# A fused graph network on one core: pair 1's GRU products in the plain form

## The chip, the cores and the metric

The kernel runs on one core of a Trainium2 chip. The metric is the device time of one execution in microseconds (us); times are medians over several runs. The engines are PE (TensorE, with its weight loads shown as PEld), DVE (VectorE), ACT (ScalarE), POOL (GpSimd), and SP (SyncE), which here only issues DMAs.

## The reference

64 graphs of 256 nodes with 256 features each (float32), and a 0/1 adjacency matrix per graph. Four layers, each a normalization, a ReLU and a residual around one graph network: three of attention, and one gated graph network of three steps, which alone matters here:

```
for i in range(3):
    m = einsum('bnd,de->bne', h, weight[i])
    aggr = einsum('bst,bsd->btd', A, m)
    h = gru_cell(aggr, h, w_ih, w_hh, b_ih, b_hh)
# gru_cell
r = sigmoid(i_r + h_r); z = sigmoid(i_z + h_z)
n = tanh(i_n + r * h_n)
h = (1 - z) * n + z * h
```

Here `i_r, i_z, i_n` are the three thirds of `aggr @ w_ih.T + b_ih`, and `h_r, h_z, h_n` those of `h @ w_hh.T + b_hh`.

## The kernel before, in words

**Units.** `graphs(u, first, nb)` states the work of one unit. There are 33: u=0 is graph 0 alone (nb=1), u=1 to 31 are pairs of graphs (nb=2), u=32 is the last graph alone. For each unit it states three attention layers (`layer0`, `layer1`, `layer2`) and `gru`. Features lie on the 128 partitions in DC=2 blocks; the S = 256 nb nodes of the unit lie along the free dimension.

**What sets the order.** Nothing is issued where it is stated. Each step is an operation of a planner, `_Schedule`, with an engine, a cost in ns, the buffers that it reads and writes, and flags [...]. `paths` gives each operation a due time, backward from the end of its unit (PACE ns for two graphs). `play` runs the program forward in a model: each engine takes the ready operation that is due first, and one for whose buffers no slot is free is held back. Up to seven rounds follow, each with due times from a backward pass (`latest`) over the last plan; the plan with the shortest modelled span is issued, each engine in exactly that order. So an edit to one unit lays the whole program anew. Buffers come from classes with fixed numbers of slots (lines 893 to 903): `g` has 13, `ht3_` (the GRU's state, transposed) 2, `ag` 2, `am_r`, `hn` and `turn` 1, `sw` 3, PSUM banks 8.

**Setup.** Lines 1028 to 1048 multiply `weight[i]` into `w_ih` (`wc`, two thirds of whose columns are the r and z gates). Line 1054 forms sums and differences of gate weights: `s3` and `sh` stay in SBUF, `s[0..2]` of each layer go to DRAM (`sd`) and are fetched again as `sw` (line 1611). Setup operations have no unit of their own: they are due when the first operation that needs them is.

**A GRU layer.** `aggregate` (line 1471) multiplies the state's rows, split in a high and a low part (`hl`, line 1458), by the adjacency; the result is `ag`. Then come the gates, in one of two forms, then per block j the transposes back to rows (`rows_of`, line 1501), which feed the next layer's split.

The plain form (`plain(j, ...)`) takes each gate as it stands: for each block j twelve matmuls of S columns (`gate`, line 1486): r and z from `whh` and `wi`, n's two parts apart. Four ACT steps, five DVE steps. It needs four `g` buffers and four banks for each j, and writes the new state to another `ht3_` buffer, `h_new`.

The shared form uses that a pair holds two right-hand sides, and takes seven block products for eight, as in Strassen's scheme:
- `t1` is the difference of the two graphs' states (one DVE step).
- `hidden` (matmuls at line 1566) forms n's hidden part: three differences on DVE (line 1563), seven matmuls of 256 columns, four ACT steps, three additions on DVE.
- `products` (matmuls at line 1623) forms r and z: three `sw` loads on SP, three differences (line 1615), seven products of four 256-column matmuls each, three ACT copies, three additions.
- `unit(j, ...)` ends the gates: one 512-column gate (two matmuls), five ACT steps of which four are of one graph, four DVE steps; the state is written in place.

Steps issued through the helper `vec` show line 913 in the profile, whatever they are.

Of the kernel before, what the change touches and what calls it, by code (L numbers as in the profile page):

```python
# [2 lines left out]

# [514 lines left out]
SLOPES = (0.2, 0.01, 0.2)  # L518
SPREAD = 3
PACE = 93800  # L520


def _runs(numbers):
# [22 lines left out]
class _Schedule:  # L546
# [33 lines left out]
    def buf(self, cls, shape, dtype=F32, tile=None):  # L580
        return _Buf(cls, shape, dtype, tile)
# [229 lines left out]
def _fast_path(  # L811
# [38 lines left out]
    P = 128  # L850
    DC = D // P
    C = 2 * N // P
    S = 2 * N
# [50 lines left out]
    buf, op = sched.buf, sched.op  # L904
# [7 lines left out]
    def vec(fn, cost, *args, reads=(), writes=(), engine="dve", port=False, **kw):  # L912
        emit = lambda: fn(*[a() if callable(a) else a for a in args], **kw)  # L913
        op(engine, cost, emit, reads, writes, port=port)
# [173 lines left out]
    def graphs(u, first, nb):  # L1088

        C = 2 * nb  # L1090
        S = nb * N
# [44 lines left out]
        def transposed(xn, cls):  # L1136
            ht = buf(cls, [P, DC, S])

            def block(dc):
                ps = bank()  # L1140

                def emit():
                    for c in range(C):
                        nc.tensor.transpose(  # L1144
                            ps.tile[:, c * P : (c + 1) * P], xn.tile[:, c, dc * P : (dc + 1) * P], ident
                        )

                op("pe", pe(445), emit, [xn], [ps], takes=[ht])
                vec(nc.scalar.copy, act(600), lambda: ht.tile[:, dc, :], lambda: ps.tile[:, :S],
                    reads=[ps], writes=[(ht, dc)], engine="act")  # L1150

            for dc in range(DC):
                block(dc)
            return ht
# [294 lines left out]
        def gru(pair):  # L1449
# [65 lines left out]
            ht = transposed(hn, "ht3_")  # L1515
# [2 lines left out]
                aggregate(ag, split(lambda dc=dc: hn.tile[:, :, dc * P : (dc + 1) * P], [hn], True), dc)  # L1518
            for i in range(L):
                last = i == L - 1  # L1520
                h_new = ht if nb == 2 else buf("ht3_", [P, DC, S])
                wi = wc[:, i]
                stt = nc.vector.scalar_tensor_tensor

# [158 lines left out]
                        op0=OP.mult, op1=OP.subtract, reads=[d, n], writes=[(ht, j)], port=True)  # L1683

                half = 0.5 if i == 0 else 0.25
                if nb == 2:
                    t1 = buf("g", [P, DC, N])
                    vec(nc.vector.tensor_tensor, 700, lambda t1=t1: t1.tile, lambda ht=ht: ht.tile[:, :, N:],
                        lambda ht=ht: ht.tile[:, :, :N], op=OP.subtract, reads=[ht], writes=[t1], port=True)
                    ns = hidden(ht, t1)  # L1690
                    rz = products(i, ht, t1, ag, wi)
                    for j in range(DC):
                        unit(j, ht, ag, wi, half, ns[j], *rz)
                else:
                    for j in range(DC):
                        plain(j, ht, ag, h_new, wi, half)
# [5 lines left out]
                ht = h_new  # L1702
# [4 lines left out]
        layer1(pair)  # L1707
        layer2(pair)
        gru(pair)


    for u, (first, nb) in enumerate(units):
        sched.group = u
        sched.end[u] = (first + nb) * PACE / 2
        graphs(u, first, nb)
# [3 lines left out]
    sched.group = U  # L1719
    sched.end[U] = sched.end[-1] = (B / 2 + 1) * PACE  # L1720
    good, bad = buf("rs", [P, 64]), buf("rs", [P, 1])
# [66 lines left out]
```

## Time and profile before

| | |
|---|---|
| median of 3 runs | 3045.0 us (3042.98 to 3045.96) |
| the profiled execution | 3046.62 us, its span 3044.8 us |
| PE busy | 2974.3 us |
| DVE busy | 2606.7 us |
| ACT busy | 2124.8 us |
| granted PE clock, mean | 0.991 |

A line of the profile names the source line, the engine, the operation, and "out<-in" by tile names without their numbers: `bank` is PSUM, `pt` attention weights, `ht` the transposed features or state, `ag` the aggregate, `g` a scratch tile. Busy time is the union of an engine's instructions; matmuls are pipelined, so their durations overlap. Each float32 matmul of the program is two MATMUL records. A wait is put down to what ended last before the waiting instruction started. Windows count from the start of the span.

Where the early units stand: the first GRU product of pair 1 (u=1) is at 149.6 us on PE, those of graph 0 (u=0) at 174.7 us where they need only the state, and at 247 us where they need its aggregate, those of pair 2 (u=2) from about 298 us.

### The profile page before, as it was taken

To read this page: it belongs to the slowest core of one execution; us is meant where nothing else is said; L and a number is where in the kernel's file an instruction comes from. 1 tells how busy PE (TensorE), PEld (TensorE's weight loads), DVE (VectorE), ACT (ScalarE), POOL (GpSimd) and SP (SyncE) were. 2 spreads that over 40 slices of the span, in tenths; PEclk is the share of its full clock that TensorE was granted. 3 is DMA by queue.
4 is the path that set the end of the run, shared out by engine and by line. 5 is a ranking of instruction groups with operands and counts; after the bars stand their busy time and mean duration, and the time that the engine had idled before them with its cause. 6 is when DMAs were issued, how large, how long until landed. Compare 5 with 4: busy or idle time off the path is not lost.

```text
span 3044.8 us, 58325 instructions
## 1 busy us (share of the span) xinstructions
PE 2974.3 (98%) x21458; PEld 2478.7 (81%) x21458; DVE 2606.7 (86%) x6310; ACT 2124.8 (70%) x4997; POOL 425.4 (14%) x643
## 2 busy tenths in 40 slices
PE   8699999999999999999999999999999999999998
PEld 7588787888888888888888888888888888888887
DVE  7877788988988888988888988888988888988774
ACT  7566577776777776677777777777777777776554
POOL 3301101111111011111011111011111011111000
PEclk9799999999999999999999999999999999999999
DMA  5111122212212212212222222211222221211110
GB/s 146 40 62 44 55 81 78 81 54 84 74 64 84 84 54 80 74 65 83 84 67 69 72 67 84 84 70 64 70 70 81 84 72 62 67 63 59 49 42 28
DMA packets 150946, 212.56 MB, mean 70 GB/s; under 512 B 49238, under 2 KB 102012, under 8 KB 143228
## 3 DMA queue, kind: packets, MB, share of 16 engines
q1 hardware_dynamic: 146752, 207.40, 21.3%
q8 instruction: 172, 2.82, 0.4%
q10 hardware_dynamic: 3900, 1.34, 0.2%
q14 instruction: 122, 1.00, 0.1%
HBM read 180.62 MB, written 19.68 MB: 66 GB/s over the span
## 4 chain that ended last, share of the span: by engine, by line
PE 90%; DVE 6%; ACT 1%; DMA 1%; POOL 1%; SPq 1%; issue 0%; ACTq 0%; DVEq 0%; POOLq 0%
PE bank L1623 34%; PE bank L1486 12%; PE bank L1166 11%; PE bank L1275 11%; PE bank L1566 9%; PE bank L1471 6%; PE bank L1144 4%; PE bank L1501 3%; DVE o L913 1%; DVE g L913 1%; DVE pt L913 1%; SPq L1352 1%; PE bank L1203 1%; DMA sw<-sd 1%; ACT pt L1256 1%; DVE mean L913 0%
## 5 line engine op out<-in xcount | busy, mean ns | idle before, releaser
L913 ACT ACTIVATE g<-bank,bg 128x256 f32<-128x256 f32 (+1 forms) x780 | 395.3, 522 | 222.0 <-PE bank L1623 100.1
L1256 ACT ACTIVATE pt<-cb,f 128x256 f32<-128x256 f32 x1062 | 465.0, 504 | 99.9 <-PE bank L1275 99.6
L913 DVE SCALAR_TENSOR_TENSOR pt<-pt,f,cap 128x256 f32<-128x256 f32 x1152 | 487.7, 477 | 18.1 <-ACT pt L1256 12.8
L1275 PEld LDWEIGHTS bank<-wh,pt 128*64 128x64 f32 (+1 forms) x8704 | 347.7, 141 | 73.5 <-issue 46.7
L1275 PE MATMUL bank<-wh,pt 128*64 128x65 f32 (+1 forms) x8704 | 396.0, 232 | 7.5 <-DVE pt L913 6.7
L1486 PE MATMUL bank<-ag,wc 128*128 128x512 f32 (+1 forms) x888 | 383.1, 561 | 0.0
L913 ACT ACTIVATE g<-g,bg 128x256 f32<-128x256 f32 x570 | 267.1, 502 | 133.3 <-DVE g L913 105.2
L1623 PE MATMUL bank<-g,sw 128*128 128x256 f32 x1488 | 351.5, 379 | 0.0
L913 ACT COPY g<-bank 128x512 f32<-128x512 f32 x279 | 163.1, 585 | 252.0 <-PE bank L1623 234.3
L1623 PEld LDWEIGHTS bank<-g,sw 128*128 128x128 f32 x1488 | 282.7, 190 | 38.6
L1486 PEld LDWEIGHTS bank<-ag,wc 128*128 128x128 f32 x888 | 160.6, 190 | 106.9 <-issue 95.4
L1118 POOL TENSOR_SCALAR mv<-mv 128x4 f32<-128x4 f32 (+1 forms) x132 | 48.0, 364 | 1409.9 <-DVE mv L1110 1131.3
L1471 PE MATMUL bank<-am_r,hl 128*128 128x256 f32 x1536 | 235.1, 299 | 0.8 <-DVE am_r L913 0.4
L913 DVE TENSOR_TENSOR g<-bank,g 128x512 f32<-128x512 f32 x279 | 190.3, 683 | 37.4 <-PE bank L1623 20.7
L1127 ACT ACTIVATE xn<-xt,mv 128x256 f32<-128x256 f32 x384 | 208.9, 598 | 10.9 <-DVE mv L913 10.5
L1109 DVE BATCH_NORM_STATS2 st<-xt 128x6 f32<-128x256 f32 x512 | 208.6, 407 | 7.7 <-DMA xt<-in_x_dram 7.4
L1471 PEld LDWEIGHTS bank<-am_r,hl 128*128 128x128 f32 x1536 | 202.4, 189 | 10.6 <-DVE hl L913 1.1
L1623 PE MATMUL bank<-ag,sw 128*128 128x256 f32 x744 | 179.1, 384 | 7.7 <-DVE g L913 4.1
L1623 PE MATMUL bank<-ag,wc 128*128 128x256 f32 x744 | 179.4, 384 | 0.7 <-ACT ag L913 0.7
L1623 PE MATMUL bank<-ht,whh 128*128 128x256 f32 x744 | 178.7, 384 | 0.8 <-ACT ht L913 0.8
L1623 PE MATMUL bank<-g,s 128*128 128x256 f32 x744 | 176.1, 380 | 0.0
L1623 PE MATMUL bank<-g,wc 128*128 128x256 f32 x744 | 175.9, 379 | 0.0
(128 smaller groups left out, 5892.7 us busy)
## 6 DMA issues: line engine op xcount, KB each, us to landing
sw<-sd SPq DMA_DIRECT2D x279, 256.0 KB, 2.6
cb<-rd SPq DMA_DIRECT2D x58, 1024.0 KB, 4.6
xt<-in_x_dram SPq DMA_DIRECT2D x31, 512.0 KB, 3.7
at<-in_adj_dram SPq DMA_DIRECT2D x31, 512.0 KB, 6.0
out_dram<-xt SPq DMA_DIRECT2D x31, 512.0 KB, 3.0
cb<-rd SPq DMA_DIRECT2D x29, 256.0 KB, 3.3
sd<-g SPq DMA_DIRECT2D x9, 256.0 KB, 2.3
cap<-cap_n SPq DMA_TRANSPOSE x128, 2.4
```

Source lines behind the costliest of these rows:

```text
L913: emit = lambda: fn(*[a() if callable(a) else a for a in args], **kw)
L1109: nc.vector.bn_stats(st.tile[:, c, :], xt.tile[:, c, :])
L1127: op("act", 610, lambda: nc.scalar.activation(xn.tile[:, c, :], xt.tile[:, c, :], AF.Relu, bias=mv.tile[:, 3, c : c + 1], scale=mv.tile[:, ...
L1144: nc.tensor.transpose(ps.tile[:, c * P : (c + 1) * P], xn.tile[:, c, dc * P : (dc + 1) * P], ident)
L1166: nc.tensor.matmul(ps.tile[:, : heads * W], lhsT=ht.tile[:, dc, c * P : (c + 1) * P], rhs=we[:, dc].rearrange("p h w -> p (h w)"), start=( ...
L1256: op("act", 500, lambda: nc.scalar.activation(pt.tile[:, b, jc, :], source(h, b), AF.Exp, scale=slope - 1.0, bias=f.tile[:, 1, h, c : c + ...
L1275: nc.tensor.matmul(ps[q * Q : (q + 1) * Q], lhsT=pt.tile[:, b, jc, i0 : i0 + Q], rhs=wh.tile[:, h, 2 * b + jc, :w], start=(jc == 0), stop= ...
L1471: nc.tensor.matmul(ps.tile[:, b * N : (b + 1) * N], lhsT=hl.tile[:, k, 2 * b + sc, :], rhs=am.tile[:, 2 * b + sc, :], start=(k == 0 and sc ...
L1486: nc.tensor.matmul(ps.tile[:, :S], lhsT=w[:, dc, g * P : (g + 1) * P], rhs=v.tile[:, dc, :], start=(first and dc == 0), stop=(last and dc ...
L1501: nc.tensor.transpose(ps.tile[:, c * P : (c + 1) * P], ht.tile[:, j, c * P : (c + 1) * P], ident)
L1566: op("pe", 432, lambda: nc.tensor.matmul(ps.tile[:, where], lhsT=w, rhs=v(), start=first, stop=False, skip_group_check=True,), [*reads, B_ ...
L1623: nc.tensor.matmul(ps.tile[:, j * N : (j + 1) * N], lhsT=w()[:, dc, j * P : (j + 1) * P], rhs=view()[:, dc], start=(first and j == 0 and d ...
```

## The change

The pair u=1 takes the plain form in all three GRU layers, with S = 512, and a second `ht3_` buffer for its new state. Pairs u=2 to 31 keep the shared form; graphs 0 and 63 were plain already. The setup is unchanged, but its sums are first needed by u=2. The added import is not used.

```diff
+import random
...
 SPREAD = 3
 PACE = 93800
+PLAIN = 2
...
             for i in range(L):
                 last = i == L - 1
-                h_new = ht if nb == 2 else buf("ht3_", [P, DC, S])
+                h_new = ht if nb == 2 and u >= PLAIN else buf("ht3_", [P, DC, S])
                 wi = wc[:, i]
...
                 half = 0.5 if i == 0 else 0.25
-                if nb == 2:
+                if nb == 2 and u >= PLAIN:
                     t1 = buf("g", [P, DC, N])
...
                     ns = hidden(ht, t1)
                     rz = products(i, ht, t1, ag, wi)
                     for j in range(DC):
                         unit(j, ht, ag, wi, half, ns[j], *rz)
                 else:
                     for j in range(DC):
                         plain(j, ht, ag, h_new, wi, half)
```

## The prediction, made before the changed kernel was run

> **What bounds the kernel now.** I read the page first (busy times, the 40 slices, the granted clock), then the waits of PE, then windows of the first 500 us, then the timeline of the longest gap.
>
> ```profile
> span 3044.8 us, 58325 instructions
> ...
> PE 2974.3 (98%) x21458; PEld 2478.7 (81%) x21458; DVE 2606.7 (86%) x6310; ACT 2124.8 (70%) x4997; POOL 425.4 (14%) x643
> ...
> PE   8699999999999999999999999999999999999998
> ...
> PEclk9799999999999999999999999999999999999999
> ```
>
> PE (TensorE) is idle for 3044.8 - 2974.3 = 70.5 us in all, and the slices put nearly all of that into the first two or three (76 us each). The windows of 500 us from 1000 to 2500 have PE busy 499.2, 498.7 and 498.9. So a microsecond of PE work added anywhere lengthens the kernel by a microsecond, unless a gap takes it up, and the gaps worth having lie before 500 us. The change concerns graphs 1 and 2 (unit u=1), and their GRU stands in just that region: its first product on PE starts at 149.6 us, the last write of its state is at about 321. The windows there (columns: stretch; busy PE, PEld, DVE, ACT, POOL; granted clock; DMA share; GB/s):
>
> ```profile
> core 0: us, PE busy (x) PEld busy (x) DVE busy (x) ACT busy (x) POOL busy (x), PEclk, DMA share, GB/s
> ...
> 150.00:160.00 10.00, 10.00 (x48) 8.78 (x48) 9.79 (x24) 5.65 (x12) 2.98 (x6) 1.00 0.38 133
> 160.00:170.00 10.00, 7.74 (x92) 6.54 (x91) 9.93 (x27) 10.00 (x26) 0.00 (x0) 1.00 0.22 55
> ...
> 220.00:228.00 8.00, 7.93 (x98) 6.84 (x97) 7.93 (x25) 4.01 (x10) 0.00 (x0) 1.00 0.07 26
> 228.00:233.00 5.00, 0.00 (x0) 0.00 (x1) 5.00 (x14) 5.00 (x14) 0.00 (x0) 0.88 0.00 2
> 233.00:240.00 7.00, 6.33 (x18) 5.07 (x19) 6.81 (x19) 4.08 (x14) 1.52 (x2) 0.50 0.01 2
> ...
> 320.00:334.00 14.00, 10.88 (x43) 7.02 (x42) 12.37 (x32) 5.79 (x12) 3.33 (x3) 1.00 0.17 43
> ```
>
> The reader is to see that where PE stops, DVE (VectorE) is full: 9.79 and 9.93 of 10 us around the gap at 163 us, 5.00 of 5 in the gap at 228, and that the clock is 0.50 after the longer gap. The waits of PE over the whole kernel (total us, times, longest):
>
> ```profile
> PE bank L1144 <- ACT xn L1127: 30.6, 2, 16.8
> ...
> PE bank L1566 <- ACT ag L913: 5.1, 1, 5.1
> ...
> PE bank L1623 <- DMA sw<-sd: 3.1, 6, 0.7
> ```
>
> The 30.6 us are the load at the very start (13.8) and the gap from 88 to 105 us (16.8), both before this GRU. The 5.1 us are one wait of pair 1's GRU, and the timeline of ACT, DVE and PE shows what stands in it:
>
> ```profile
> 225.52 6.48 ACT L1256 ACTIVATE pt<-cb,f 128x256 f32<-128x256 f32 x16
> ...
> 232.37 0.57 ACT L913 COPY ag<-bank 128x512 f32<-128x512 f32 x1
> ```
>
> ```profile
> 226.41 6.42 DVE L913 SCALAR_TENSOR_TENSOR pt<-pt,f,cap 128x256 f32<-128x256 f32 x16
> ...
> 233.94 0.69 DVE L913 TENSOR_TENSOR hl<-bank,hl 128x512 fp32r<-128x512 f32 x1
> ```
>
> ```profile
> 233.00 2.08 PE L1566 MATMUL bank<-ht,whh 128*128 128x256 f32 x4 [5.07 <-ACT ag L913]
> ```
>
> Sixteen attention weights of a later pair sit on ACT and DVE ahead of the two small steps that feed the third GRU layer, and PE has nothing else ready.
>
> [...]
>
> **The change, part by part.** Three layers of one pair leave the shared form (`hidden`, `products`, `unit`) for `plain`. Each product is two records in the trace. From the chain of work:
>
> ```profile
> 195.23 1.73 PE bank L1623 x8
> ...
> 210.45 3.43 PE bank L1486 x8
> ```
>
> A 256-column record takes 1.73/8 = 0.216 us, one of 512 columns 3.43/8 = 0.429.
>
> PE: the shared form has 7 products of four 256-column matmuls (56 records), `hidden` 7 matmuls (14) and two 512-column gates (8): 70 x 0.216 + 8 x 0.429 = 18.6 us. Plain has 24 matmuls of 512 columns, 48 x 0.429 = 20.6. Added: 2.0 us a layer, **6.1 us** in all. This is certain, and hidden only if it fills a gap.
>
> DVE and ACT, from the groups (the second number after the bar is the mean ns of one):
>
> ```profile
> L913 DVE TENSOR_TENSOR g<-bank,g 128x512 f32<-128x512 f32 x279 | 190.3, 683 | 37.4 <-PE bank L1623 20.7
> ...
> L1563 DVE TENSOR_TENSOR g<-ht,g 128x256 f32<-128x256 f32 x6 | 2.5, 412 | 0.0
> ```
>
> ```profile
> L913 ACT ACTIVATE g<-g,bg 128x256 f32<-128x256 f32 x18 | 8.5, 501 | 3.4 <-DVE g L913 3.4
> ...
> L913 ACT ACTIVATE g<-bank,bg 128x512 f32<-128x512 f32 x4 | 2.7, 687 | 3.0 <-PE bank L1486 3.0
> ```
>
> DVE per layer: shared 15 steps of 512 elements and 6 of 256, 15 x 0.684 + 6 x 0.415 = 12.8 us; plain 10 x 0.684 = 6.8. Saved 5.9, or 5.0 if each is counted by its distance to the next (0.60 and 0.33): **15 to 18 us** in three layers. ACT per layer: shared 6 x 0.470 + 6 x 0.501 + 2 x 0.687 + 3 copies x 0.585 = 9.0; plain 6 x 0.687 and two from SBUF, which the trace lacks at 512 elements (I take 0.72[...]): 5.6. Saved 3.4, **10 us** in all. Neither engine ends the kernel, so this is worth only what it closes of PE's gaps.
>
> What it closes. (a) DVE issues three of the sums for the weight differences (L1054) at 105 to 107 us inside a DVE-led piece of the chain. Pair 1 no longer needs them, so they can fall later: 3 x 0.60 = 1.8 us, at least 0. (b) Between 149 and 165 us DVE is full, with 4.3 us of layer 0's differences and additions by 160 us; plain has at most two steps (1.2) there, so some 3 us less, and the 2.26 us gap goes: 2.3. (c) The gap at 228: 5.07 us, 0.67 at 237, and the half clock behind it (4 records in 2.08 for 0.86, 8 aggregates in 1.72 for 0.94, 16 records in 5.97 for 3.46): 4.5 us. Together 10.3. With 10 to 12 us less DVE work before it, in two layers, the weights can stand ahead of the layer's end instead of inside it. I take all of it; zero is the other end, because the order is the planner's and not DVE's load. Sum: 6.1 - 1.8 - 2.3 - 10.3 = **-8.3 us**.
>
> Costed at nothing: nine `sw` loads on SP (256 KB, 2.6 us to land) and the wait for them. PE's waits from 105 to 500 us name no `sw`, so nothing shortens[...]. The state: plain writes h_new to another of two `ht3_` slots. The single graph 0 already does so while pair 1 holds the other slot, and its two final writes then stand together (262.2, 280.5, 297.5 us), waiting for the last reader of the old state: a few tenths of a us of DVE order, hidden while PE has other pairs' attention. If that cover is gone, it is the second rival of the slower side.
>
> The working is against the profiled execution (3046.62 us, span 3044.8). The median of the runs shown is 3045.0, 1.6 us (0.05%) lower; I put the difference on the median: 3045.0 - 8.3 = 3036.7, so **3037**.
>
> **The rivals.** First, the gaps move but half remain: the planner lays the whole program anew, and a wait like (c) appears at another place. For it: the 320 to 334 us window and 473 us show more such gaps, in pairs that don't change. Against: DVE's load does fall. (a), (b) and a quarter of (c) cover the 6.1: about 3045. Second, slower: PE has its fill anyway. From 170 to 228 us PE is idle under 0.1 us, so the added work there is paid in full, and if (c) is an order and no load, nothing pays it back: 3045 + 6.1 = 3051; it decides if the GRU's aggregation still stands behind a block of 16 weights. Third, the slots: pair 2's transposes already come at 307 us, though its split was at 286.8. If pair 1 in plain form holds both slots, pair 2's GRU isn't there as filler; one more gap like (c) costs 9.6 us or so on top: 3061. That the edit does nothing is excluded: the test on `u` is plainly met by unit 1.
>
> **How the numbers follow.** Chances: forecast 0.45 (own range 3028 to 3041, the low end if the gap after 320 us, 3.7 us and its half clock, goes too), half remain 0.22, full price 0.18, slots 0.15. A difference under 0.2% (6 us) can't be told from none. Faster by more: 0.45 less 0.05 above 3039, 0.40. Within: 0.05 + 0.22 + 0.04 = 0.31. Slower: 0.14 + 0.15 = 0.29. The range from 3028 to 3057 leaves out most of the slot case and a little below.
>
> **What would show it.** PE busy up by some 6 us less the half-clock time; DVE down 15 to 18, ACT about 10; `sw` loads 270 for 279[...]. I am wrong if the gap between two layers of pair 1 is still there, if a longer gap stands elsewhere before 500 us, or if the early gap at 88 us changes: I have left that alone, since nothing of this GRU runs before it.

## The result, and the profile after

The changed kernel takes 3016.94 us (median, 3014.51 to 3018.15) against 3044.55 us of the kernel before beside it: ratio 0.9907, 95% interval 0.9892 to 0.9923, some 28 us faster. The forecast was 3037 in a range from 3028 to 3057: the direction was right, the size a third of what was measured, and the time lies below the range.

From the page of the kernel after, these lines answer to those shown of before (line numbers are 2 higher than before):

```profile
span 3016.3 us, 58014 instructions
...
PE 2971.5 (99%) x21368; PEld 2454.4 (81%) x21368; DVE 2595.9 (86%) x6277; ACT 2118.2 (70%) x4970; POOL 425.8 (14%) x643
...
PE   8899999999999999999999999999999999999998
...
PEclk9899999999999999999999999999999999999999
```

PE is idle for 3016.3 - 2971.5 = 44.8 us, 25.7 less than the 70.5 of before. Its busy time fell by 2.8 us although the plain form adds 6.1 us of work; that leaves 8.9 us, put down to less time at a granted clock of 0.50. In windows of 1 us it is 0.50 from 89 to 112, 137 to 143, 232 to 242, 335 to 341 and 475 to 477 us before, and from 86 to 88, 113 to 116 and 120 to 129 us after; its mean is 0.996 for 0.991. The windows bear this out as an estimate: PE's busy time times the missing share of the clock, summed over windows up to 600 us, is some 15 us before and 5 after. 25.7 + 2.8 = 28.5, the difference of the spans.

The same windows as in the prediction, of the kernel after:

```profile
core 0: us, PE busy (x) PEld busy (x) DVE busy (x) ACT busy (x) POOL busy (x), PEclk, DMA share, GB/s
...
160.00:170.00 10.00, 10.00 (x60) 8.50 (x59) 8.30 (x35) 8.21 (x19) 3.72 (x7) 1.00 0.01 2
...
228.00:233.00 5.00, 5.00 (x29) 4.23 (x28) 5.00 (x11) 4.45 (x10) 4.69 (x4) 1.00 0.16 34
233.00:240.00 7.00, 7.00 (x43) 5.32 (x42) 6.86 (x19) 2.61 (x6) 1.25 (x2) 1.00 0.08 16
...
320.00:334.00 14.00, 14.00 (x45) 8.36 (x44) 13.29 (x35) 6.22 (x11) 6.66 (x6) 1.00 0.07 20
```

All gaps that the prediction wanted closed are closed, and the one at 320 us too. But the waits of PE show a second change, which the prediction had left out (total us, times, longest one):

```profile
PE bank L1146 <- ACT xn L1129: 17.5, 5, 9.7
...
PE bank L1625 <- DMA sw<-sd: 2.2, 6, 0.8
```

The wait for `xn`, the normalized input, is 13 us shorter (30.6 before), and the single gap of 16.8 us is gone. It stood at 88 to 105 us, long before pair 1's GRU. It is not gone without a trace: one wait for `xn` of 7.3 us now stands at 116 us. Coarser windows, first of the kernel before, then of the one after, show how the gain is spread:

```profile
80.00:140.00 60.00, 36.02 (x357) 30.21 (x354) 50.86 (x152) 28.33 (x69) 19.66 (x25) 0.77 0.15 46
140.00:240.00 100.00, 91.98 (x656) 76.76 (x655) 82.45 (x208) 71.01 (x172) 13.16 (x19) 0.94 0.16 51
240.00:345.00 105.00, 100.01 (x695) 84.03 (x695) 82.74 (x201) 61.87 (x146) 19.73 (x26) 0.96 0.16 46
345.00:600.00 255.00, 249.83 (x1864) 206.98 (x1863) 214.57 (x525) 184.18 (x438) 33.17 (x52) 0.99 0.24 77
```

```profile
80.00:140.00 60.00, 44.94 (x422) 36.85 (x421) 56.21 (x160) 36.92 (x96) 22.74 (x33) 0.86 0.11 36
140.00:240.00 100.00, 99.83 (x792) 77.23 (x791) 82.75 (x233) 73.55 (x174) 18.61 (x23) 1.00 0.11 36
240.00:345.00 105.00, 105.00 (x654) 74.68 (x653) 75.62 (x178) 64.43 (x145) 13.21 (x18) 1.00 0.16 51
345.00:600.00 255.00, 254.06 (x1885) 210.38 (x1884) 224.72 (x544) 189.55 (x448) 35.68 (x55) 1.00 0.24 77
```

Idle time of PE fell by 8.9 us between 80 and 140, 7.9 between 140 and 240, 5.0 to 345 and 4.2 to 600. From 600 us on both kernels run alike (2295.35 and 2295.24 us busy of the 2300 us to 2900).

What else differs shows in the timeline of ACT: the casts that open a unit's GRU (`hl<-hn`). A pair's tile has 512 elements, a single graph's 256. In a line, the first number is the start and the second the duration, in us. Before:

```profile
144.19 0.60 ACT L1458 CAST hl<-hn 128x512 fp32r<-128x512 f32 x1
...
237.30 0.71 ACT L1458 CAST hl<-hn 128x256 fp32r<-128x256 f32 x2
```

After:

```profile
127.42 0.41 ACT L1460 CAST hl<-hn 128x256 fp32r<-128x256 f32 x1
...
204.81 0.61 ACT L1460 CAST hl<-hn 128x512 fp32r<-128x512 f32 x1
```

Graph 0 and pair 1 have changed places.

**Why they change places.** The planner's first due times follow a rule (`paths`): an operation is due when its successor is, less 3.43 times the successor's cost, less 1100 ns.

```
late = min(late, due[s.index] - self.STRETCH * s.cost - self.MARGIN)
```

In the shared form the longest path through one GRU layer of a pair has 17 steps with 14,595 ns of cost: 3.43 x 14.595 + 17 x 1.1 = 68.8 us. In the plain form it has 12 steps with 9,445 ns: 45.6 us. Three layers make 69.5 us. Counted back in this way from its end, pair 1's first step is due at -298.2 us before and at -228.8 after; graph 0's is at -248.9 in both. So before, pair 1 is due 49.3 us ahead of graph 0 and takes its place at the head of the queues; after, graph 0 is due 20.1 us ahead. I call this distance the lead of graph 0: -49 us before, 20 us after. It belongs to the first due times; the plan that is issued can come from a later round.

### The profile page after: what moved, and what is told of

Its sections match the earlier page's. It is cut to its first block, busy times and chain, and to the rows that moved or that the text cites. A ratio compares the mean times of both kernels' runs of the same rounds, so it can differ in the third digit from the quotient of the medians.

```text
span 3016.3 us, 58014 instructions
## 1 busy us (share of the span) xinstructions
PE 2971.5 (99%) x21368; PEld 2454.4 (81%) x21368; DVE 2595.9 (86%) x6277; ACT 2118.2 (70%) x4970; POOL 425.8 (14%) x643
## 4 chain that ended last, share of the span: by engine, by line
PE 93%; DVE 4%; DMA 1%; ACT 1%; SPq 1%; POOL 1%; issue 0%; ACTq 0%; DVEq 0%; POOLq 0%
PE bank L1625 34%; PE bank L1488 14%; PE bank L1168 11%; PE bank L1277 11%; PE bank L1568 9%; PE bank L1473 6%; PE bank L1146 4%; PE bank L1503 3%; DVE g L915 1%; DVE o L915 1%; SPq L1354 1%; DMA sw<-sd 1%; DVE pt L915 1%; PE bank L1035 1%; POOL cap_n L1344 0%; PE bank L1221 0%
## 5 line engine op out<-in xcount | busy, mean ns | idle before, releaser
L1488 PE MATMUL bank<-ag,wc 128*128 128x512 f32 (+1 forms) x936 | 406.5, 563 | 0.0
L915 ACT ACTIVATE g<-g,bg 128x256 f32<-128x256 f32 (+1 forms) x558 | 262.0, 503 | 121.0 <-DVE g L915 101.6
L1625 PE MATMUL bank<-g,sw 128*128 128x256 f32 x1440 | 339.9, 379 | 0.0
L1625 PEld LDWEIGHTS bank<-g,sw 128*128 128x128 f32 x1440 | 273.3, 190 | 37.6 <-issue 0.5
L1488 PEld LDWEIGHTS bank<-ag,wc 128*128 128x128 f32 x936 | 168.5, 190 | 112.3 <-issue 101.4
L1625 PE MATMUL bank<-ag,wc 128*128 128x256 f32 x720 | 172.2, 382 | 0.1
L1625 PE MATMUL bank<-ht,whh 128*128 128x256 f32 x720 | 170.4, 380 | 0.0
```

The lines of the kernel that those rows point to most:

```text
L1488: nc.tensor.matmul(ps.tile[:, :S], lhsT=w[:, dc, g * P : (g + 1) * P], rhs=v.tile[:, dc, :], start=(first and dc == 0), stop=(last and dc ...
L1625: nc.tensor.matmul(ps.tile[:, j * N : (j + 1) * N], lhsT=w()[:, dc, j * P : (j + 1) * P], rhs=view()[:, dc], start=(first and j == 0 and d ...
```

## Theories and experiments

- **Order**: the plain form acts by turning the due times of graph 0 and pair 1. Graph 0 then goes first; the thought was that its GRU fills PE while pair 1 is in its attention layers.
- **Load**: the prediction's reason. The plain form saves DVE and ACT work in pair 1's GRU, and PE's gaps close.
- **Draw** (chance): any edit lays the whole order anew; this one was lucky.

Ratios are to runs of the kernel before on the same chip.

**Form and order apart, two by two.** The other two corners, besides the kernels before and after, change only where the due times start. The first, on the kernel before:

```diff
         sched.end[u] = (first + nb) * PACE / 2
+        if u == 0:
+            sched.end[u] -= 60000
```

Expected: 

> Pair 1 keeps the shared form; only the end from which graph 0's due times are counted back is 60 us earlier, so that graph 0's first step is due before pair 1's, as it is in the changed kernel. Order theory (the plain form acts by making pair 1 due later than graph 0, and so lets graph 0 go first): the gain is there without the plain form, about 3011 to 3022 us (the changed kernel's 3017, less up to 6 us of PE work). Load theory (the gain is the DVE and ACT work that the plain form saves in pair 1's GRU): as before, 3040 to 3050. Draw theory (any edit lays the whole order anew and this one was lucky): anywhere from 3010 to 3065.

Measured: 3020.97 us, ratio 0.992 (0.9904 to 0.9937). The shared form with graph 0 first has nearly the whole gain. Its windows:

```profile
80.00:140.00 60.00, 46.29 (x389) 38.63 (x384) 41.22 (x123) 36.97 (x95) 16.06 (x26) 0.86 0.22 71
140.00:240.00 100.00, 93.03 (x806) 79.02 (x804) 89.20 (x240) 71.14 (x171) 16.12 (x23) 0.98 0.14 43
```

The second, on the changed kernel, has `if u == 1` in the same place. Expected: 

> The changed kernel, with the end from which pair 1's due times are counted back 60 us earlier, so that pair 1 is due before graph 0 again, in the plain form. Order theory: the gain goes, 3038 to 3055 us. Load theory: the gain stays, 3012 to 3022. Draw theory: anywhere from 3010 to 3065.

Measured: 3049.29 us, ratio 1.0002 (0.9993 to 1.0011). The plain form with pair 1 first has nothing of the gain. Its timeline of ACT has pair 1 and graph 0 in the order of before:

```profile
143.23 0.61 ACT L1460 CAST hl<-hn 128x512 fp32r<-128x512 f32 x1
...
226.69 0.41 ACT L1460 CAST hl<-hn 128x256 fp32r<-128x256 f32 x1
```

Its windows from 80 us on show the gap of 80 to 140 us back (37.35 us busy). The idle time from 140 to 240 us is closed here too (1.8 us, for 8.0 before), but 4.5 us more of it stand between 345 and 600 us:

```profile
80.00:140.00 60.00, 37.35 (x381) 30.09 (x376) 51.61 (x160) 28.53 (x71) 18.11 (x26) 0.77 0.09 26
140.00:240.00 100.00, 98.21 (x598) 64.97 (x599) 60.17 (x145) 65.94 (x153) 13.33 (x20) 0.97 0.12 40
240.00:345.00 105.00, 100.40 (x666) 78.66 (x665) 89.41 (x226) 61.05 (x140) 19.01 (x24) 0.97 0.13 39
345.00:600.00 255.00, 245.30 (x1804) 203.09 (x1805) 213.64 (x522) 184.39 (x438) 31.89 (x48) 1.00 0.25 76
```

So the form and the order act in different places. With graph 0 first, PE idles less from 80 to 140 us and from 345 to 600 us, in both forms (345 to 600: 0.3 us for 5.2 in the shared form, 0.9 for 9.7 in the plain one). With the plain form, it idles less from 140 to 240 us, in both orders (1.8 us for 8.0 with pair 1 first, 0.2 for 7.0 with graph 0 first). Only the first is worth time. The gap of pair 1's third layer shows it best. The two casts that open that layer, before:

```profile
223.99 0.58 ACT L1458 CAST hl<-bank 128x512 fp32r<-128x512 f32 x1 [6.46 <-PE bank L1501]
...
231.91 0.56 ACT L1458 CAST hl<-bank 128x512 fp32r<-128x512 f32 x1
```

and in the plain form with pair 1 first (in brackets ACT's idle time before the step, and what ended it):

```profile
222.08 0.58 ACT L1460 CAST hl<-bank 128x512 fp32r<-128x512 f32 x1 [0.60 <-PE bank L1503]
...
224.97 0.57 ACT L1460 CAST hl<-bank 128x512 fp32r<-128x512 f32 x1
```

Of the 16 weights between them six are left, and PE has no wait over 0.6 us from 142 to 305 us. The gap that the prediction priced highest is gone, and the time is that of before.

The two corners also answer a rival: in the plain form the setup's sums for the shared form are first needed by pair 2 instead of pair 1. That is so in the second corner, which has no gain, and not in the first, which has it.

**The same with one planner round.** To take the draw out, the four corners with only the first plan, whose order follows the due times directly:

```diff
-    ROUNDS = 7
+    ROUNDS = 1
```

Expected of the shared form, pair 1 first: 

> The kernel before with only the first of the planner's seven rounds, so that no later round can improve or spoil one of the four of this set by chance. Slower than the kernel before, by about 1%: 3065 to 3090 us on every theory. It is the base of the set.

Of the shared form, graph 0 first: 

> One round, shared form, graph 0 due 60 us earlier and so ahead of pair 1. Order theory: 18 to 30 us below the base of the set. Load theory: as the base, within 6 us. Draw theory: no relation, since each first round is a draw of its own.

Of the plain form, pair 1 first: 

> One round, pair 1 in the plain form but due 60 us earlier and so ahead of graph 0. Order theory: as the base, within 8 us. Load theory: 15 to 30 us below the base. Draw theory: no relation.

Of the plain form, graph 0 first: 

> The changed kernel with one round. Order theory: as the shared form with graph 0 first, within 8 us. Load theory: as the plain form with pair 1 first. Both: the lowest of the four, by more than the order alone gives. Draw theory: no relation.

| one round | pair 1 first | graph 0 first |
|---|---|---|
| shared form | 1.0161 (1.0144 to 1.0178) | 1.0096 (1.0079 to 1.0113) |
| plain form | 1.0152 (1.0135 to 1.0169) | 1.0103 (1.0086 to 1.012) |

The medians are 3097.06, 3077.43, 3094.74 and 3079.24 us. The order is worth 0.65% in the shared form and 0.49% in the plain one; the form is worth -0.09% and +0.07%, both inside the intervals. With seven rounds the order is worth 0.8% in the shared form and 0.95% in the plain one; the form is worth +0.02% with pair 1 first and -0.13% with graph 0 first. So the saved load by itself is out as the cause, and so is a draw that has no relation to form and order. The base itself was 7 us slower than expected.

**Load at a fixed order.** Two runs leave every engine's order as it is, since the planner isn't told of the edit. In the first, on the kernel before, pair 1's differences and partial additions emit nothing and the products read `ht` and `ag`:

```diff
+                def kept_out(emit):
+                    return (lambda: None) if u == 1 else emit
...
-                        return op("dve", 700, lambda: nc.vector.tensor_tensor(
-                            out.tile, x_(), y_(), op=OP.subtract), reads, [out], takes, port=True)
+                        return op("dve", 700, kept_out(lambda: nc.vector.tensor_tensor(
+                            out.tile, x_(), y_(), op=OP.subtract)), reads, [out], takes, port=True)
```

Expected: 

> The kernel before, every engine in exactly its order, but for pair 1 the 13 DVE steps per GRU layer that form differences and add partial products are left out (the products read the state and the aggregate instead, and pair 1's result is therefore not the reference's): 7 x 0.68 + 6 x 0.42 = 7.3 us of DVE a layer, 22 in all, more than the plain form saves, and the waits for these steps with them. Load theory: most of the gain, 3015 to 3027 us. Order theory: little, 3034 to 3044. Draw theory: as the order theory, since the order is the same.

Measured: 3046.21 us, ratio 0.9998 (0.9989 to 1.0006). Nothing beyond 0.1%, less even than the order theory had allowed (3034 to 3044), though DVE's busy time fell by 15.8 us (2606.7 to 2590.9). The gap that the prediction priced highest stays to the tenth, and so does the early one (in this run lines 1566 and 1623 of before are 1573 and 1630, and line 1529 is a helper that the edit adds):

```profile
PE bank L1144 <- ACT xn L1127: 30.7, 2, 16.8
...
PE bank L1573 <- ACT ag L913: 5.1, 1, 5.1
```

The smaller gap at 163 us does close. It was a wait of 2.3 us for DVE before,

```profile
PE bank L1623 <- DVE g L913: 4.1, 3, 2.3
```

and the longest of this kind is 1.0 us here:

```profile
PE bank L1630 <- DVE g L1529: 1.9, 2, 1.0
```

But PE only comes to the 5.1 us gap earlier: it ends at 231.35 us for 233.00. In both traces ACT, in its fixed order, waits 6.46 us before the first of the two casts shown above, with the 16 weights behind it. The run takes out DVE's part of the load alone; ACT's steps are all there.

In the second, on the changed kernel, two DVE steps of each block of pair 1 (`d` and `h_new`) are issued three times over:

```diff
+                def often(*a, **kw):
+                    for _ in range(3 if u == 1 else 1):
+                        stt(*a, **kw)
```

Expected: 

> The changed kernel in exactly its order, but for pair 1 two DVE steps of each block are issued three times (four more a block, 24 in all, 24 x 0.60 to 0.68 = 14 to 16 us: what the plain form saved on DVE). Load theory: half of the gain or more comes back, 3030 to 3045 us. Order theory: little, 3016 to 3023.

Measured: 3037.77 us, ratio 0.9969 (0.9957 to 0.9982). This went against the order theory: DVE's busy time rose by 16.3 us, and 0.9969/0.9907 = 1.0063 is 19 us of time, two thirds of the gain. The waits of PE say where part of it is (line 1529 is the helper here):

```profile
PE bank L1146 <- ACT xn L1129: 19.4, 8, 9.8
PE bank L1503 <- DVE ht L1529: 9.1, 5, 2.7
```

The wait of the transposes for the new state is 9.1 us, for 2.7 in the changed kernel. In all, PE's idle time is 13.5 us longer than in the changed kernel and its busy time 6.0 us. The added steps stand at the end of each layer, in an order planned without them. So the run shows that DVE time added there costs its full price and more; it doesn't show that the saved time is what made the gain, since the shared form, planned with all its DVE steps, reaches 0.992 with graph 0 first. How much of the 19 us is the place of the steps and how much their sum wasn't taken apart.

**Does the order have to turn, and does a greater lead pay?** Four more starts of the due times: graph 0's end 20 us earlier (shared), pair 1's 10 us earlier (plain), graph 0's 80 us earlier (shared), and 80 us with 10 us for pair 1 (plain).

```diff
         sched.end[u] = (first + nb) * PACE / 2
+        sched.end[u] -= {0: 80000, 1: 10000}.get(u, 0)
```

Expected of the first: 

> Shared form, graph 0's end 20 us earlier. Counted by the planner's rule pair 1 is due 49 us ahead of graph 0 in the kernel before, so 20 us don't turn the order. Order theory: as before, 3040 to 3055 us. A theory that any earlier due time of graph 0 helps: a third of the gain, 3030 to 3038. Draw theory: 3010 to 3065.

Of the second: 

> The changed kernel with pair 1's end 10 us earlier. Graph 0 is due 20 us ahead there, so 10 us don't turn the order. Order theory: the gain stays, 3012 to 3024 us. Draw theory: 3010 to 3065.

Of the third: 

> Shared form, graph 0's end 80 us earlier: graph 0 is due 31 us ahead. Order theory: at least the gain of the changed kernel, 3000 to 3022 us, without the plain form. Load theory: 3040 to 3050.

Of the fourth: 

> The changed kernel with graph 0's end 80 us earlier and pair 1's 10 us, so that graph 0 is due 90 us ahead of pair 1. Order theory: a further lead of graph 0 helps as long as its GRU fills PE while pair 1 is in its attention layers: 2995 to 3015 us, below the changed kernel. If the lead is spent once graph 0 is ahead at all: 3015 to 3022.

| form, moved ends | lead of graph 0 | median us | ratio (95% interval) |
|---|---|---|---|
| shared, graph 0 by 20 us | -29 us | 3040.97 | 0.9979 (0.9972 to 0.9987) |
| plain, pair 1 by 10 us | 10 us | 3021.39 | 0.9915 (0.9898 to 0.9931) |
| shared, graph 0 by 80 us | 31 us | 3010.31 | 0.9879 (0.9863 to 0.9896) |
| plain, graph 0 by 80, pair 1 by 10 us | 90 us | 3003.96 | 0.9859 (0.9843 to 0.9875) |

While the lead is negative, 0.2% is the most that came (a new plan's luck or the nearer due time, not told apart; 3040.97 us lies at the edge of what the order theory expected); where it is positive, at least 0.8%. That the order has to turn isn't shown by this, as no lead between -29 and 10 us was tried. Seen by its size, the shared form's ratio falls rather steadily: by 0.10%, 0.15% and 0.20% for each 10 us, from -49 through -29 and 11 (the first corner, 0.992) to 31 us. A shared form with graph 0 early beats the changed kernel by 0.3% (0.9879 for 0.9907), and the fourth beats both kernels, by 1.4% and 0.5% (0.9859/0.9907). The fourth's windows show that the early stretch gains most: 53.22 us of PE work between 80 and 140 us, for 36.02 before and 44.94 after.

```profile
80.00:140.00 60.00, 53.22 (x475) 46.79 (x476) 54.24 (x149) 43.30 (x112) 20.44 (x27) 0.91 0.18 59
140.00:240.00 100.00, 98.62 (x769) 73.78 (x768) 85.10 (x237) 71.23 (x170) 19.16 (x28) 1.00 0.13 41
```

What fills that stretch differs. In the fourth run 13 us of PE's busy time from 80 to 127 us are GRU products of graph 0 (lines 1473 and 1488). In the changed kernel PE has none before 131.9 us: there it is attention work that closes the gap, so the GRU as filler is not what the order theory's gain rests on at that place. Which of the reordered attention steps frees PE wasn't taken apart.

## Why the prediction was wrong

**Right: where the time lies.** PE bounds the kernel, and only gaps before 600 us could pay: from 600 to 2900 us the two kernels differ by 0.1 us of PE's busy time. But the slices did not show that nearly all of the 70.5 us stand at the front: up to 228 us there are 40.6, and 9.4 after 2900. The work on PE (+6.1 us) can't be read alone from a busy time that also holds time at a clock of 0.50; the count of records bears it out (90 fewer, as 78 x 3 narrow and wide ones make room for 48 x 3 wide ones). The `sw` loads fell from 279 to 270, and PE's wait for them from 3.1 to 2.2 us.

**Wrong in size: DVE and ACT.** I forecast 15 to 18 us less on DVE and 10 on ACT. Measured: 10.8 (2606.7 to 2595.9) and 6.6 (2124.8 to 2118.2). Busy time joins overlapping instructions, and DVE's overlap (at 150 us of before, steps of 0.68 us start 0.60 us apart), so the lower count by distances (15) was the better one, and still too high. The 0.72 us taken for an ACT step of 512 elements from SBUF is an estimate that answers to 0.687 us of one from PSUM plus the 0.031 us by which the step from SBUF is longer at 256 elements (0.502 for 0.471). Measured after: 0.723.

**The step that failed: "What it closes", as a price.** The sum took the length of the closed gaps, with the granted clock of 0.50 behind the longest of them (233 to 242 us), as time saved; behind the 2.26 us gap at 163 us the clock was 1.00 (160 to 180 us). It counted (a) 1.8, (b) 2.3 and (c) 10.3 us against 6.1 of added work. The corner with the plain form and pair 1 first has just this: (b) and (c) are closed, and its ratio is 1.0002, not 0.997. In its profiled execution PE is idle for 69.2 us for 70.5 before, as the idle time comes back after 345 us, and PE's busy time is 7.4 us longer. So closing these gaps paid for the added work and no more.

The reason given for (c), that with less DVE work "the weights can stand ahead of the layer's end instead of inside it", does not hold in the order of before: with 15.8 us of DVE taken out, that wait is 5.1 us as it was. In plans laid for the plain form it is gone, with either unit first. Whether the lower load or the shorter path lets the planner do so isn't taken apart. For (b) the reason holds: less DVE work closes that wait in the old order too. In (a), the sums did not fall later: they all start by 71.1 us, for 106.8 before.

**The step that was missing.** An edit to one unit lays the whole program anew: the description of the kernel says so, and the prediction used this only as a source of bad luck. The due times that steer it could be counted from the code, as above: 69.5 us on pair 1's path turn 49.3 us behind into 20.1 us ahead for graph 0. With that, the gap at 88 us is no longer outside of the change. The prediction said "I have left that alone, since nothing of this GRU runs before it", and so put at nothing the place from which 8.9 of the 25.7 us of idle time came. That the direction was right is luck: the faster time came from the order, on which the forecast did not rest.

The planner's own model had it. Its modelled span for the plan that it issues is a number of the code and needs no chip: 3058.4 us before and 3036.3 after, 3038.6 and 3060.7 for the two corners, and 3057.9, 3037.8, 3019.7 and 3015.1 for the four starts in the order of the table. The measured differences from the kernel before agree with those of the model within 7 us.

**The rivals.** That half of the gaps remain, since a wait appears at another place: not in the changed kernel, where none over 0.2 us is left from 140 to 345 us, but it describes the form by itself, with pair 1 first. That PE's fill is paid in full: no, the form by itself is at 1.0002 and not 6 us slower. The slots of `ht3_`: not seen; pair 2's split is at 282.5 us, 3.7 us earlier than before.

What stays open: why a longer lead of graph 0 goes on paying in both forms, and how much of it is a lucky plan. Neighbouring starts with the same sign differ by 0.4% in the shared form (0.992 at 60 us, 0.9879 at 80).

## What to carry to other kernels

Where a planner lays out the program, an edit to one piece can change its priority against all others; here it did so through the length of its path. Count the due times before and after, see which neighbours trade places, and compare the planner's modelled spans. Test it by moving the priority alone, with the piece as it was. A closed gap is worth its length only if the time doesn't come back as idle time elsewhere; with the form alone PE was idle for 69.2 us, for 70.5 before. To learn what load is worth, keep the order fixed and take the load out; here that gave nothing (0.9998).

## What the runs showed that was not expected

16.3 us of DVE time put at the ends of three layers of one pair, in an order planned without it, cost 19 us of 3017, on an engine that is busy 86% of the time and is not the bound. Taking 15.8 us out of the same pair at the order of before gave nothing within 0.1%: of the waits of PE, the one of 2.3 us for DVE went, and the one of 5.1 us, which the order of ACT's steps makes, stayed.
